# Cross-attention and FFN kernel: other PSUM banks for the last group's transposes, two softmax divisions on another engine

## The chip, the cores and the metric

The kernel runs on one core of a Trainium2 chip. The metric is the device time of one execution in microseconds (us); before the change its median over three executions was 541.05 us (540.98 to 541.4). A core has five engines that each work through a queue of their own in order: TensorE (PE in the profile; its weight loads are the row PEld), VectorE (DVE), ScalarE (ACT), GpSimd (POOL) and SyncE (SP, which here only issues transfers). They wait for each other by semaphores. TensorE writes its results to PSUM, here eight banks of 128 partitions x 512 float32; VectorE and ScalarE read them from there[...].

## The reference

Everything is float32. x is 2 x 2048 x 512, the context 2 x 128 x 512, with 16 heads of 32.

```python
h = layernorm(x)
q = h @ wq + bq; k = ctx @ wk + bk; v = ctx @ wv + bv      # 16 heads of 32
score = einsum('bhqd,bhkd->bhqk', q, k) / sqrt(32) * mask
score = where(score == 0, -1e9, score)
x = x + einsum('bhqk,bhkd->bqhd', softmax(score), v) @ wo + bo
y = real(ifft(fft(layernorm(x)) @ w_complex)) + bias
out = x + y
```

The kernel folds the two transforms and the complex matrix into one real 512 x 512 matrix m_ffn at its start.

## The kernel before

The 4096 rows of x are eight groups of four tiles of 128 rows. For each tile, TensorE computes the scores of all 16 heads against the 128 keys into two allocations of PSUM (two banks each), one for each half of the heads. The class Softmax handles one half (128 x 8 x 128): `masked` (VectorE, L334) multiplies scores by the mask into an SBUF tile w; `maxima` (VectorE, L341 to L344) replaces zeros and finds the row minima of the negated scores; `exponentials` (ScalarE, L350) makes eight activations with their sums; `divided` takes the reciprocal of the sums on VectorE (L362) and multiplies w by it on GpSimd (L363).

`transposed_weights` (L369) then turns the weights with TensorE, head group g by head group g (four transposes of 128 x 128 into one bank), and a copy moves each bank to pt in SBUF. Each g takes two heads from the first half and two from the second, in that order, so its third transpose is the first that needs the second half's division. `context` (L392) multiplies pt with v for a whole group of tiles, `Project` the result with wo; its `evict` adds to the residual x, to which `output_bias` (GpSimd, L418) has added bo. `ffn_statistics`, `ffn_norm` (L453; a norm on VectorE, L217, and the addition of bf on GpSimd, L458) and `ffn_transposes` (L461) prepare the second part, and `Ffn` multiplies by m_ffn, adds (VectorE, L503) and stores.

PSUM is divided into three pools: ps_sc with two allocations of two banks for scores, ps_tp with two of one bank for transposes, ps_mm with two of one bank for everything that accumulates. An allocation is handed out anew when its last reader is done.

The order of the work on each engine is the order in which the code issues it; no planner changes it. While a tile's softmax runs on VectorE, ScalarE and GpSimd, TensorE does the projections and FFN of earlier groups and the transposes of the tile before. In the helper `slot` (L720), `mid_a` is work issued behind the first matmul chain of a tile and ahead of the transposed weights of the tile before; at that place `masked` of the first half has been issued, and that of the second not. The last group (index 7) is written out by hand from L1092 on, without `slot`, except for its tile 0. There is no scores work to fill TensorE behind its tile 3, so the transposes of that tile's weights, the contexts, the projections and the FFN of the group follow each other alone:

```python
    w[1].exponentials()
    f_p[2].pe(between=[(ffn_transposes, p, 3, nc.vector)])
    f_p[2].evict()
    w[1].divided()
    output_bias(last)
    run(f_p[3])
```

For the last weights the kernel takes two allocations of ps_sc and uses each one's two banks for two head groups (L1158 to L1162); copies alternate between ScalarE (g = 0, 2) and VectorE (g = 1, 3).

Of the kernel before, what the change touches and what calls it, by code (L numbers as in the profile page):

```python
# [9 lines left out]
FP = mybir.dt.float32  # L10
# [4 lines left out]
P = 128  # L15
# [7 lines left out]
def kernel(  # L23
# [34 lines left out]
    nc = tc.nc  # L58
# [5 lines left out]
    NC = D // P  # L64
    NR = P // DH
# [10 lines left out]
    ps_sc = ctx.enter_context(  # L76
        tc.tile_pool(name="ps_sc", bufs=2, space=bass.MemoryType.PSUM)
    )
    ps_tp = ctx.enter_context(
        tc.tile_pool(name="ps_tp", bufs=2, space=bass.MemoryType.PSUM)  # L80
    )
    ps_mm = ctx.enter_context(
        tc.tile_pool(name="ps_mm", bufs=2, space=bass.MemoryType.PSUM)
    )
    HD = D // 2
    HC = NC // 2
# [91 lines left out]
    nc.sync.dma_start(bf, ffn_b.partition_broadcast(P))  # L178


    def transpose_rows(dst, src, name, eng, spare=False):

        pool, tag = (ps_mm, "mm") if spare else (ps_tp, "tp")
        ps = pool.tile([P, NC, P], FP, tag=tag, name=f"tp_{name}")
        for c in range(NC):
            nc.tensor.transpose(ps[:, c, :], src[:, c * P : (c + 1) * P], ident)  # L186
        if eng is nc.scalar:
            nc.scalar.copy(dst, ps)  # L188
        else:
            eng.tensor_copy(dst, ps)  # L190
# [77 lines left out]
    def query_transposes(i, t):  # L268
        if t == 0:
            xnTs[i] = big_tile("xnT", 1, f"xnT_{i}")  # L270
        transpose_rows(
            xnTs[i][:, :, t * P : (t + 1) * P], rels[i][t], f"a{i}_{t}", nc.scalar
        )
# [50 lines left out]
    class Softmax:  # L324
# [31 lines left out]
                    accum_out=self.den[:, h : h + 1],  # L356
                )

        def divided(self):
            w = self.w  # L360
            rden = small.tile([P, HH], FP, tag="rden", name=f"rden_{self.n}")
            nc.vector.reciprocal(rden, self.den)  # L362
            nc.gpsimd.tensor_tensor(  # L363
                w, w, rden.unsqueeze(2).to_broadcast([P, HH, K]), ALU.mult
            )

# [47 lines left out]
    def output_bias(i):  # L414

        xs = groups[i]
        for t in range(TG):
            nc.gpsimd.tensor_tensor(xs[:, t, :], xs[:, t, :], bo, ALU.add)  # L418
# [39 lines left out]
        nc.gpsimd.tensor_tensor(xt, xt, bf, ALU.add)  # L458
        norms[i, t] = n

    def ffn_transposes(i, t, eng=nc.scalar, spare=False):  # L461
        nTs[i, t] = work.tile([P, NC, P], FP, tag="nT", name=f"nT_{i}_{t}")
        transpose_rows(nTs[i, t], norms.pop((i, t)), f"f{i}_{t}", eng, spare)

# [250 lines left out]
    def begin(i, t):  # L715
        sc = scores(i, t)
        weights[i, t] = [Softmax(i, t, hf, sc[hf]) for hf in range(2)]
        return weights[i, t]
# [124 lines left out]
    w = begin(0, 0)  # L843
# [20 lines left out]
    w = begin(0, 1)  # L864
# [21 lines left out]
    w = begin(0, 2)  # L886
# [19 lines left out]
    w = begin(0, 3)  # L906
# [32 lines left out]
    w = begin(1, 0)  # L939
# [29 lines left out]
    for i in range(1, last - 1):  # L969
        p, pp, n, nn = i - 1, i - 2, i + 1, i + 2  # L970
# [12 lines left out]
        if i > 1:  # L983
            load_rows(nn)
            load_mask(n)
            load_residual(p)
            slot(
                i,
                0,
                [f_pp[1], f_pp[2], q[1]],  # L990
                turned=(p, TG - 1),
                early=[(ffn_transposes, pp, 2)],
                pool=[(relative, nn, t, nc.gpsimd) for t in range(TG)],
                on_b=[(ffn_norm, pp, 3), (query_statistics, nn, 0, 2)],
                on_c=[(query_statistics, nn, 2, TG)],
                end=[(context, p, 0, 2)],
            )
# [3 lines left out]
            second,  # L1001
            turned=(i, 0),
            early=[(context, p, 2, NC)] + if_pp((ffn_transposes, pp, 3)),
            pool=[(output_bias, p)],
            on_b=[(query_norm, nn, 0), (query_norm, nn, 1)],
# [8 lines left out]
            on_b=[(ffn_norm, p, 0), (query_norm, nn, 2), (query_norm, nn, 3)],  # L1014
            on_c=[(ffn_statistics, p, 1)],
            end=[(ffn_transposes, p, 0)],
        )
        slot(
# [14 lines left out]
    i, n, p, pp = last - 1, last, last - 2, last - 3  # L1033
# [4 lines left out]
    f = [Ffn(pp, t) for t in range(TG)]  # L1038
# [17 lines left out]
        pool=[(output_bias, p)],  # L1056
# [12 lines left out]
        [o[2], o[3], f_p[0]],  # L1069
        turned=(i, 2),  # L1070
        pool=[(ffn_norm, p, 0)],
        mid_a=[(ffn_transposes, p, 0)],
        on_a=[(ffn_statistics, p, 1)],
        on_b=[(ffn_norm, p, 1), (ffn_statistics, p, 2), (ffn_statistics, p, 3)],
        end=[(ffn_transposes, p, 1)],
# [1 line left out]
    i, p, pp = last, last - 1, last - 2  # L1077
    o = [Project(p, t) for t in range(TG)]
    f = f_p
# [5 lines left out]
        turned=(p, TG - 1),  # L1085
        late=True,
        pool=[(ffn_norm, pp, 2)],
        mid_a=[(ffn_transposes, pp, 2)],
        on_a=[(ffn_norm, pp, 3)],
        mid_c=[(ffn_transposes, pp, 3, nc.scalar, True)],  # L1090
    )
    w = begin(i, 1)  # L1092
    w[0].masked()
# [17 lines left out]
    old = w  # L1111
    w = begin(i, 2)
    w[0].masked()
    old[1].divided()
    o[1].pe()
    w[0].maxima()
    ffn_norm(p, 0)
# [17 lines left out]
    w = begin(i, 3)  # L1135
# [16 lines left out]
    w[1].exponentials()  # L1152
    f_p[2].pe(between=[(ffn_transposes, p, 3, nc.vector)])
    f_p[2].evict()
    w[1].divided()
    output_bias(last)
    run(f_p[3])
    free = [  # L1158
        ps_sc.tile([P, 2, NC, K], FP, tag="sc", name=f"tpw_last_{hf}")
        for hf in range(2)  # L1160
    ]
    banks = [free[g // 2][:, g % 2] for g in range(NC)]  # L1162
    for g in range(NC):
        transposed_weights(
            last, TG - 1, g, g + 1, nc.vector if g % 2 else None, banks
# [3 lines left out]
    f = [Ffn(last, t) for t in range(TG)]  # L1169
# [56 lines left out]
```

## Time and profile before

| | |
|---|---|
| median of three executions | 541.05 us |
| the profiled execution | 541.23 us |
| its span, first to last instruction | 539.0 us |
| TensorE clock granted | 1.00 |
| TensorE, VectorE, ScalarE, GpSimd busy | 98, 81, 64, 61% of the span |
| scores of group 7, tile 0 | from 439.90 us |
| first context matmul of group 7 | 502.51 us |

In rows of the timeline, the columns are the start in us from the span's start, the duration in us, engine, line, operation, the tile written and the tiles read with their shapes, and how many instructions were merged into the row; in brackets stands the idle time of the engine just before, and what ended it. A chain of waits is followed back from the last instruction: each step goes to what released it. Its rows have start, duration, engine and what.

By stages: from 441.0 to 452.5 VectorE is busy for 11.24 of 11.5 us; from 465 to 482 TensorE for 16.04 of 17.0; from 482 to 497 TensorE for 15.0 of 15.0 and VectorE for 13.34; from 497 to 502.5 TensorE for 3.86 of 5.5; from 502.5 to 539 TensorE for 33.15 of 36.5.

### The profile page before, as it was taken

The numbers are of one execution on the slowest core, as the hardware profiler recorded it, in microseconds if no ns is written. First come the engines' busy times: TensorE is split into PE (matmuls) and PEld (weight loads), VectorE is DVE, ScalarE is ACT, GpSimd is POOL, SyncE is SP. The second block draws the span as 40 slices with busy tenths as digits, with TensorE's granted clock in tenths as the row PEclk, the third lists the DMA queues.
The fourth block names the chain that finished last, engine by engine and source line by source line (L and its number), as shares of the span: only waits on it lengthen the run. The fifth ranks groups of instructions, "written<-read, shape, count | busy, mean of one in ns | idle before, by whom it ended". The sixth has DMA issues, their size and how long they took to land.

```text
span 539.0 us, 8776 instructions
## 1 busy us (share of the span) xinstructions
PE 526.0 (98%) x3005; PEld 293.4 (54%) x3005; DVE 437.2 (81%) x617; ACT 342.3 (64%) x1299; POOL 330.0 (61%) x268
## 2 busy tenths in 40 slices
PE   8979999999999999999999999999999999999897
PEld 7745567455545555455545555455545554455344
DVE  4698888799987998879887998879967898987251
ACT  3376786676677676666677676666676667666210
POOL 3246768935895459735895459735764466866450
PEclk9999999999999999999999999999999999999999
DMA  8960203000510015000610015000312001201002
GB/s 309 385 224 0 76 4 99 1 0 2 195 41 2 19 52 184 0 21 1 196 40 0 21 51 184 1 21 0 118 41 76 23 20 48 91 1 60 19 0 79
DMA packets 22992, 36.49 MB, mean 68 GB/s; under 512 B 2202, under 2 KB 6562, under 8 KB 22948
## 3 DMA queue, kind: packets, MB, share of 16 engines
q1 hardware_dynamic: 22260, 34.75, 18.7%
q10 hardware_dynamic: 688, 1.18, 0.6%
q8 instruction: 24, 0.39, 0.3%
q14 instruction: 20, 0.16, 0.1%
HBM read 27.53 MB, written 8.39 MB: 67 GB/s over the span
## 4 chain that ended last, share of the span: by engine, by line
PE 83%; DVE 10%; ACT 3%; POOL 2%; issue 1%; POOLq 0%; ACTq 0%; DVEq 0%
PE o L200 20%; PE q L200 16%; PE y L200 16%; PE tpw L380 9%; PE c L402 6%; PE sc L315 5%; PE tp_f L186 3%; PE tp_a L186 3%; ACT w L350 2%; DVE w L341 2%; DVE w L334 2%; DVE nmax L343 2%; POOL w L363 1%; PE k L547 1%; PE v L200 1%; DVE st_a L209 1%
## 5 line engine op out<-in xcount | busy, mean ns | idle before, releaser
L350 ACT ACTIVATE w<-w,nmax 128x128 f32<-128x128 f32 x512 | 198.3, 395 | 16.0 <-DVE nmax L344 15.0
L363 POOL TENSOR_TENSOR w<-w,rden 128x1024 f32<-128x1024 f32 x64 | 123.9, 1935 | 84.9 <-DVE rden L362 69.3
L200 PE MATMUL o<-wo,cT 128*128 128x512 f32 x256 | 115.3, 594 | 0.0
L200 PE MATMUL q<-xnT,wq 128*128 128x512 f32 (+1 forms) x256 | 112.0, 582 | 2.6 <-ACT qT L293 1.5
L200 PE MATMUL y<-m_ffn,nT 128*128 128x512 f32 x248 | 112.0, 594 | 0.2 <-DVE x L503 0.2
L387 ACT COPY pt<-tpw 128x512 f32<-128x512 f32 x120 | 64.3, 587 | 60.0 <-PE tpw L380 60.0
L350 ACT ACTIVATION_READ_ACCUMULATOR w<-w,nmax 128x1 f32 x512 | 99.2, 194 | 0.0
L341 DVE SCALAR_TENSOR_TENSOR w<-w 128x1024 f32<-128x1024 f32 x64 | 88.8, 1387 | 0.9
L334 DVE TENSOR_TENSOR w<-sc,mask 128x1024 f32<-128x1024 f32 x64 | 77.5, 1212 | 13.9 <-PE sc L315 13.6
L343 DVE TENSOR_REDUCE nmax<-w 128x8 f32<-128x1024 f32 x64 | 78.1, 1220 | 2.2
L380 PEld LDWEIGHTS tpw<-ident,w 128*128 128x128 f32 x496 | 57.7, 141 | 33.6 <-issue 29.3
L200 PEld LDWEIGHTS q<-xnT,wq 128*128 128x128 f32 x256 | 46.3, 190 | 48.6 <-issue 40.2
L200 PEld LDWEIGHTS o<-wo,cT 128*128 128x128 f32 x256 | 46.2, 190 | 47.5 <-issue 46.1
L200 PEld LDWEIGHTS y<-m_ffn,nT 128*128 128x128 f32 x248 | 44.6, 190 | 44.6 <-issue 43.8
L380 PE MATMUL tpw<-ident,w 128*128 128x128 f32 x496 | 65.2, 273 | 2.0 <-POOL w L363 1.0
L458 POOL TENSOR_TENSOR x<-x,bf 128x512 f32<-128x512 f32 x32 | 50.4, 1576 | 15.0 <-DVE norm_f L217 15.0
L213 POOL TENSOR_SCALAR rstd_f<-mv_f 128x1 f32<-128x1 f32 x32 | 18.1, 564 | 67.0 <-DVE mv_f L210 67.0
L418 POOL TENSOR_TENSOR x<-x,bo 128x512 f32<-128x512 f32 x32 | 46.9, 1494 | 0.0
L234 POOL TENSOR_SCALAR rel<-rows 128x512 f32<-128x512 f32 x26 | 42.2, 1638 | 1.4 <-PE tp_a L186 1.4
L315 PEld LDWEIGHTS sc<-kT,qT 32*128 32x128 f32 x1024 | 31.5, 186 | 15.1 <-issue 12.8
L188 ACT COPY nT<-tp_f 128x512 f32<-128x512 f32 x29 | 16.9, 583 | 34.3 <-PE tp_f L186 34.2
L362 DVE RECIPROCAL rden<-den 128x8 f32<-128x8 f32 x64 | 12.6, 197 | 31.9 <-ACT w L350 31.7
(99 smaller groups left out, 550.6 us busy)
## 6 DMA issues: line engine op xcount, KB each, us to landing
rows<-in_x_dram SPq DMA_DIRECT2D x32, 256.0 KB, 4.3
x<-in_x_dram SPq DMA_DIRECT2D x32, 256.0 KB, 5.1
out_dram<-x SPq DMA_DIRECT2D x31, 256.0 KB, 2.0
mask<-in_mask_Bx1xSxS_fk_dram SPq DMA_DIRECT2D x8, 256.0 KB, 5.8
wk<-in_L_xattn_wk_w_dram ACTq DMA_DIRECT2D x2, 512.0 KB, 6.3
wq<-in_L_xattn_wq_w_dram SPq DMA_DIRECT2D x1, 1024.0 KB, 7.8
wr<-n_L_ffn_w_freq_real_dram SPq DMA_DIRECT2D x2, 512.0 KB, 5.2
wi<-n_L_ffn_w_freq_imag_dram SPq DMA_DIRECT2D x2, 512.0 KB, 7.4
```

The costliest lines, as they stand in the source:

```text
L200: nc.tensor.matmul(ps, lhs(c), rhs(c), start=(c == 0), stop=(c == NC - 1))
L234: eng.tensor_scalar(d, xt, xt[:, 0:1], None, ALU.subtract)
L315: nc.tensor.matmul(sc[r // 2][:, r % 2, g, :], qTs[i][rows, g, t * P : (t + 1) * P], kT[rows, g, b * K : (b + 1) * K], start=True, stop=True,)
L334: nc.vector.tensor_tensor(self.w, self.sc.rearrange("p r g k -> p (r g) k"), self.mrow, ALU.mult)
L341: nc.vector.scalar_tensor_tensor(w, w, 0.0, w, ALU.is_equal, ALU.subtract)
L343: nc.vector.tensor_reduce(self.nmax, w, AX.X, ALU.min)
L350: nc.scalar.activation(w[:, h, :], w[:, h, :], AF.Exp, bias=self.nmax[:, h : h + 1], scale=-UNIT, accum_out=self.den[:, h : h + 1],)
L363: nc.gpsimd.tensor_tensor(w, w, rden.unsqueeze(2).to_broadcast([P, HH, K]), ALU.mult)
L380: nc.tensor.transpose(ps[:, r, :], ws[r // 2].w[:, (r % 2) * NC + g, :], ident)
L387: nc.scalar.copy(dst, ps)
L418: nc.gpsimd.tensor_tensor(xs[:, t, :], xs[:, t, :], bo, ALU.add)
L458: nc.gpsimd.tensor_tensor(xt, xt, bf, ALU.add)
```

## The change

Three things change.

- In the last group, `divided` of the second half of tile 1 (L1114) and of tile 3 (L1155) multiplies on VectorE instead of GpSimd. The reciprocal was on VectorE already.
- The last tile's weights are turned through four allocations: head groups 0 and 1 take the first bank of each of two score allocations, 2 and 3 an allocation of ps_tp each.
- Two of the norm transposes, in tile 3 of group 6 (L1072) and in tile 0 of group 7 (L1088), go through the first bank of a score allocation instead of one of ps_tp. Elsewhere `spare` means what it did: none is ps_tp, and for group 5's tile 3 (L1090) it is ps_mm, now given by name.

```diff
-    def transpose_rows(dst, src, name, eng, spare=False):
-        pool, tag = (ps_mm, "mm") if spare else (ps_tp, "tp")
-        ps = pool.tile([P, NC, P], FP, tag=tag, name=f"tp_{name}")
+    def transpose_rows(dst, src, name, eng, spare=None):
+        if spare is ps_sc:
+            ps = ps_sc.tile([P, 2, NC, P], FP, tag="sc", name=f"tp_{name}")[:, 0]
+        else:
+            pool, tag = (ps_mm, "mm") if spare else (ps_tp, "tp")
+            ps = pool.tile([P, NC, P], FP, tag=tag, name=f"tp_{name}")
...
-        def divided(self):
+        def divided(self, eng=nc.gpsimd):
             w = self.w
             rden = small.tile([P, HH], FP, tag="rden", name=f"rden_{self.n}")
             nc.vector.reciprocal(rden, self.den)
-            nc.gpsimd.tensor_tensor(
+            eng.tensor_tensor(
                 w, w, rden.unsqueeze(2).to_broadcast([P, HH, K]), ALU.mult
             )
...
-        mid_a=[(ffn_transposes, p, 0)],
+        mid_a=[(ffn_transposes, p, 0, nc.scalar, ps_sc)],
...
-        mid_a=[(ffn_transposes, pp, 2)],
+        mid_a=[(ffn_transposes, pp, 2, nc.scalar, ps_sc)],
         on_a=[(ffn_norm, pp, 3)],
-        mid_c=[(ffn_transposes, pp, 3, nc.scalar, True)],
+        mid_c=[(ffn_transposes, pp, 3, nc.scalar, ps_mm)],
...
     w[0].masked()
-    old[1].divided()
+    old[1].divided(nc.vector)
     o[1].pe()
     w[0].maxima()
...
     f_p[2].evict()
-    w[1].divided()
+    w[1].divided(nc.vector)
     output_bias(last)
     run(f_p[3])
     free = [
         ps_sc.tile([P, 2, NC, K], FP, tag="sc", name=f"tpw_last_{hf}")
         for hf in range(2)
     ]
-    banks = [free[g // 2][:, g % 2] for g in range(NC)]
+    banks = [bank[:, 0] for bank in free] + [
+        ps_tp.tile([P, NR, P], FP, tag="tp", name=f"tpw_last_{g}")
+        for g in range(HC, NC)
+    ]
```

More of the change, by code (lines that the diff above doesn't have):

```diff
@@ L459, in ffn_norm, with ffn_transposes @@
         norms[i, t] = n
-    def ffn_transposes(i, t, eng=nc.scalar, spare=False):
+    def ffn_transposes(i, t, eng=nc.scalar, spare=None):
         nTs[i, t] = work.tile([P, NC, P], FP, tag="nT", name=f"nT_{i}_{t}")
```

## The prediction

> **What bounds the kernel now.** I read the busy shares first, then the chain of work that ended last, then each engine's rows in order of time around the places that the diff touches.
>
> ```profile
> PE 526.0 (98%) x3005; PEld 293.4 (54%) x3005; DVE 437.2 (81%) x617; ACT 342.3 (64%) x1299; POOL 330.0 (61%) x268
> ```
>
> TensorE is busy almost throughout, so only the places where it stands still, or where the chain leaves it, can give time. The chain through the last group:
>
> ```profile
> 468.56 2.77 POOL w L363
> ...
> 471.38 0.87 PE tpw L380 x6
> ...
> 480.88 1.11 PE sc L315 x32
> 482.01 1.22 DVE w L334
> ...
> 493.52 3.20 ACT w L350 x16
> ...
> 497.12 1.87 POOL w L363
> ...
> 499.04 0.45 PE tpw_last L380 x2
> 499.52 0.59 ACT pt L387
> ...
> 502.58 3.62 PE c L402 x32
> ```
>
> Both divisions that the change moves stand on it (468.56 and 497.12), and so do the copies between the last transposes. From 482.01 to 493.4 the chain is VectorE's queue, row after row without a gap; from 502.58 to the end it is TensorE alone. The stalls themselves, in TensorE's and VectorE's rows:
>
> ```profile
> 471.38 0.87 PE L380 MATMUL tpw<-ident,w 128*128 128x128 f32 x6 [0.96 <-POOL w L363]
> 480.38 0.20 DVE L362 RECIPROCAL rden<-den 128x8 f32<-128x8 f32 x1 [0.70 <-ACT w L350]
> 482.01 1.22 DVE L334 TENSOR_TENSOR w<-sc,mask 128x1024 f32<-128x1024 f32 x1 [1.43 <-PE sc L315]
> 499.04 0.44 PE L380 MATMUL tpw_last<-ident,w 128*128 128x128 f32 x2 [0.28 <-POOL w L363]
> 500.15 1.09 PE L380 MATMUL tpw_last<-ident,w 128*128 128x128 f32 x8 [0.68 <-ACT pt L387]
> 501.93 0.66 PE L380 MATMUL tpw_last<-ident,w 128*128 128x128 f32 x4 [0.68 <-ACT pt L387]
> ```
>
> The two 0.68s fall before g=1 and g=3. Bank 1 is the second half of the allocation that bank 0 lies in, and waits for bank 0's copy although it is another bank; the same for 3 behind 2.
>
> **Part 1, the division of tile 1's second half on VectorE (L1114).** Nothing is added but the engine changes: one 128x1024 operation with two SBUF inputs leaves POOL (2.76 us here) and enters VectorE's queue before w[0].maxima. The trace has no such multiplication on VectorE; the nearest row is L341, the same size with its inputs in SBUF, 1.21 us when POOL is quiet. Its bounds are 1.19 (fastest L341) and 2.36 (slowest, behind POOL); I take 1.20, as POOL's rows are empty from 468.16 until the next norm. It runs 468.45 to 469.65. TensorE's third transpose goes at 470.26, right behind its second, instead of 471.38: 1.12 earlier, and so through o[2] and o[3] to tile 3's scores, which end at about 480.8 instead of 481.97.
>
> Behind the division on VectorE stand maxima, the norm, masked, an addition and the statistics, all 1.2 later. L344 gives 0.32 back: it took 0.49 at 470.86 against 0.17 elsewhere, because it waited for POOL's division, now gone. So the second half's maxima end 0.84 later (477.88). ScalarE's exponentials started at 477.16 and now start at 478.0, take their 3.18 and end at 481.18; the reciprocal follows, and masked of tile 3 goes at 481.33. Gain at that point: 482.01 - 481.33 = **0.68**, not 1.12; what ends last there is ScalarE, no longer the scores. Late next on POOL: a bias addition and tile 2's two divisions, by 0.84; the second then ends at 484.23, where TensorE comes to use it at 484.15 + 0.22, so it costs nothing as long as that 0.1 holds. Bounds of this part: 1.12 gained if ScalarE were not late, and 1.2 lost if the division simply lengthened VectorE's stretch.
>
> **Part 2, the division of tile 3's second half (L1155).** POOL needed 0.14 + 1.90 behind the reciprocal (ends 496.95 and 498.99). On VectorE it costs 1.2, but POOL is now not empty: the four additions of output_bias no longer queue behind this division, and start as soon as the first half's division ends. Such a case stands in the trace, VectorE's row and then POOL's:
>
> ```profile
> 280.84 2.07 DVE L341 SCALAR_TENSOR_TENSOR w<-w 128x1024 f32<-128x1024 f32 x1
> 280.54 5.95 POOL L418 TENSOR_TENSOR x<-x,bo 128x512 f32<-128x512 f32 x4
> ```
>
> The VectorE operation waits out the first addition (1.24, a quarter of the undisturbed 4.95 at 498.94: to 281.78), then runs 1.13 to 282.91, and POOL goes on after it (5.95 instead of 4.95). Here: the first half's division ends 2.05 behind its reciprocal's end (494.10), so at 496.15; the first addition at 497.39; VectorE's division is ready at 496.97, waits 0.42 and ends at 497.39 + 1.13 = 498.52, against 498.99. But TensorE itself reaches the third transpose no sooner than 498.38 + 0.22 = 498.60, so without part 1 the gain is 499.04 - 498.60 = 0.44; with everything ahead of it moved by 0.68, f_p[3] ends 0.9 sooner and it is the division that ends last, at 498.52 - 0.68 = 497.84; with the 0.05 that its release takes, the third transpose goes at 497.89, which is 499.04 - 0.68 - 0.47: **0.47**. Bounds: 0.9 if POOL happened to be between two additions, -0.7 if it waited for a whole second one. The output bias itself ends near 501.7; its reader is the addition at 509.93, so it stays covered by 5 us.
>
> [...] by the rows an uncontended VectorE operation is 1.20 against 1.90 to 2.76, and a contended one still ends 0.47 sooner than POOL's. I take the rows.
>
> **Part 3, four allocations for the last weights (L1158).** Same instructions, other banks: 0 and 1 become the first bank of each of two score allocations, 2 and 3 the two transpose banks, whose last readers (f_p[3]'s norm copy at 494.02 and a ScalarE copy near 492) are long done. The two waits before g=1 and g=3 go. Now 499.04 to 502.51, 3.47 us, lies between the third transpose and the first context matmul. After: 14 transposes at 0.109 (eight take 0.87 in the chain) = 1.53, and 0.14 for the hand-over that the rows show (502.37 to 502.51): 1.67. Gain **1.80**. The copies must keep up: with the third transpose at T, g=0 is complete at T+0.45 and copied by ScalarE at T+1.06, before the contexts' T+1.67; g=1's copy on VectorE follows f_p[3]'s addition and ends at T+1.62, needed at T+2.6; g=3's at T+2.45, needed at T+4.4. If the copies were not ready, the cover would be 0.6 us thin for g=0, nothing else.
>
> **Part 4, two norm transposes through a score allocation (L1072, L1088).** The next transposed weights get both transpose banks and lose a wait of 0.24 at 431.13 and of 0.29 at 445.87. The wait added is for masked of the first half, over at 427.8 and 442.3, when TensorE gets there at 429.85 and 444.54. After the first, scores land 0.15 sooner (the next norm, ending 439.18, holds the rest), VectorE had 0.22 to spare before masked, and then:
>
> ```profile
> 442.85 1.52 DVE L217 TENSOR_SCALAR norm_f<-x,mv_f,rstd_f 128x512 f32<-128x512 f32 x1
> ```
>
> A norm takes 0.54 undisturbed; this one waits for POOL's division (442.19 to 444.08), whose start doesn't depend on TensorE. So it ends at 444.37 whatever comes sooner. After the second, VectorE's queue runs full from 444.29 until f[3] waits for it at 452.4. I take **0**; bounds 0 and 0.5.
>
> **Sum.** 0.68 + 0.47 + 1.80 + 0 = 2.95 on the profiled span: 539.0 to 536.05. That execution took 541.23, 0.18 above the median of 541.05, and what lies around the span doesn't change: 541.05 - 2.95 = **538.1 us**.
>
> **Rivals.**
> - *Part 1 is swallowed* (18%): VectorE's stretch from 482 is the bound, and tile 2's late POOL work runs into it: a norm and a 0.1 us cover stand next to POOL's division at 484.2. For it: contended rows of 0.4 to 1.1 us on both engines there; against: the lateness found above. Without the 0.68 it is 538.8, and 539.3 if another 0.5 of such waits comes in.
> - [...] (6%): the last division waits for more than one bias addition. One more costs 1.24 (539.3), all four 3.7 (541.8). Against it: the row at 280.84, which got in after one.
> - *The banks don't part* (4%): the waits before g=1 and g=3 stay, by another dependency. 538.1 + 1.8 = 539.9. Against: g=2, in another allocation, followed g=1 without a wait.
> - *Part 4 gives more* (6%): the 0.5 of removed waits arrives; 537.6.
> - *Slower: the score allocation that part 4 takes is the second half's* (4%). The two norm transposes would wait for the second half's masked, over at 432.77 and 448.09: stalls of 2.92 and 3.55. The first passes wholly to VectorE, which then waits for the scores; of the second 1.8 is covered by f[2]'s addition at 451.75. 2.92 + 1.75 - 2.95 gives 542.8. It decides once the stalls that pass exceed 2.95 + 1.1. Against: with two allocations in turn, and an odd one between, the one that comes next each time is the half that was read first.
>
> **Chances and range.** The forecast has 62%, its own range 537.4 to 538.7. With the swallowed part 1 and the better part 4 it makes 86%; the range to hold 8 in 10 is 537.1 to 539.6. A run tells 0.2%, 1.1 us, from no change: faster is below 539.97. The forecast, the swallowed part 1, the better part 4, the banks (just)[...] make 0.89; [...] shares of unknowns make 0.06 for no change; the slower rival and some unknown 0.05.
>
> **What would show it.** Right: VectorE rows at L363 of about 1.2 (tile 1) and 1.5 (tile 3, wait included); no wait for POOL at tile 1's transposes; tile 3's masked released by ScalarE's exponentials, about 0.7 sooner; sixteen last transposes with at most one short wait after the second, contexts 1.67 after the third; an unchanged distance from contexts to the end. Wrong: a VectorE division above 2 us, a TensorE wait of 3 us at a norm transpose, masked of tile 3 at 482 or later, or last copies on which the contexts wait.

## The result and the profile after

The changed kernel takes 538.27 us (median of six executions, 538.15 to 538.36) against 541.3 us for the kernel before on the same chip: a ratio of 0.9944, 95% interval 0.9931 to 0.9956, or 3.0 us less. The forecast was 538.1. The profiled execution has a span of 536.1 us against 539.0. Line numbers are four higher after the change (L363 is L367, L334 is L338); in each version below they follow its own edit.

The chain through the last group, from tile 1's division to the first contexts:

```profile
468.40 1.23 DVE w L367
...
472.05 0.17 DVE nmax L348
...
477.74 0.18 DVE nmax L348
...
478.03 3.20 ACT w L354 x16
...
481.25 0.20 DVE rden L366
481.46 1.09 DVE w L338
...
497.77 1.90 PE tpw_last L384 x16
499.67 3.62 PE c L406 x32
```

GpSimd has left the chain. Between tile 1's division and tile 3 the chain is now VectorE and then ScalarE; TensorE's scores, which stood in front of tile 3's masked before (480.88, then 482.01), are no longer in it. The sixteen last transposes are one piece, where the chain had three with two copies between them. From the first context matmul to the end it is 36.5 us in both kernels (502.51 to 539.0, 499.60 to 536.1).

TensorE's rows at tile 1's transposes and at the end, then GpSimd's and VectorE's around the last division:

```profile
469.99 1.04 PE L384 MATMUL tpw<-ident,w 128*128 128x128 f32 x8
...
497.61 2.06 PE L384 MATMUL tpw_last<-ident,w 128*128 128x128 f32 x16
499.60 3.69 PE L406 MATMUL c<-pt,v 128*32 128x512 f32 x32
...
495.46 5.95 POOL L422 TENSOR_TENSOR x<-x,bo 128x512 f32<-128x512 f32 x4
...
496.33 1.47 DVE L367 TENSOR_TENSOR w<-w,rden 128x1024 f32<-128x1024 f32 x1
```

The 0.96 us wait at tile 1 is gone. VectorE's division takes 1.23 where GpSimd is idle and 1.47 where it adds the bias: it starts inside the first addition, as L341 did at 280.84, and GpSimd's four additions take 5.95 instead of 4.95.

Executions differ by up to 0.7 us in when they reach the last group, through what comes ahead of it, and a row's absolute time can't be compared across kernels to better than that. Below, times in the last group are therefore counted from one row: VectorE's addition for o[0], at 465.56 before and 465.51 after, just ahead of tile 2. Counted so, by each version's profiled execution:

| kernel | tile 3's masked | third of the last transposes | first context matmul |
|---|---|---|---|
| before | 16.45 | 33.48 | 36.95 |
| changed | 15.86 | one piece | 34.09 |
| banks alone | 16.44 | 33.48 | 35.16 |
| tile 1's division alone | 15.86 | 32.88 | 36.81 (granted clock 0.50 just before) |
| tile 3's division alone | 16.45 | 33.03 | 36.48 |
| norm transposes alone | 16.45 | 33.48 | 36.95 |

### The profile page after: what moved, and what is told of

It reads as the page before. It is cut to its first block, busy times and chain, and to the rows that moved or that the text cites. A ratio compares the mean times of both kernels' runs of the same rounds, so it can differ in the third digit from the quotient of the medians.

```text
span 536.1 us, 8773 instructions
## 1 busy us (share of the span) xinstructions
PE 525.3 (98%) x3005; PEld 293.2 (55%) x3005; DVE 439.4 (82%) x619; ACT 342.2 (64%) x1299; POOL 326.5 (61%) x266
## 4 chain that ended last, share of the span: by engine, by line
PE 76%; DVE 17%; ACT 5%; POOL 1%; issue 1%; ACTq 0%; POOLq 0%; DVEq 0%
PE y L204 16%; PE o L204 16%; PE q L204 15%; PE tpw L384 8%; PE c L406 5%; PE sc L319 5%; ACT w L354 4%; DVE w L345 4%; DVE nmax L347 3%; DVE w L338 3%; PE tp_a L190 3%; PE tp_f L190 2%; PE k L551 1%; PE v L204 1%; DVE norm_f L221 1%
## 5 line engine op out<-in xcount | busy, mean ns | idle before, releaser
L367 POOL TENSOR_TENSOR w<-w,rden 128x1024 f32<-128x1024 f32 x62 | 119.3, 1924 | 83.4 <-DVE rden L366 67.2
L345 DVE SCALAR_TENSOR_TENSOR w<-w 128x1024 f32<-128x1024 f32 x64 | 88.7, 1386 | 0.9
L338 DVE TENSOR_TENSOR w<-sc,mask 128x1024 f32<-128x1024 f32 x64 | 77.4, 1211 | 12.4 <-PE sc L319 11.8
```

Of the source, the lines that this page charges most:

```text
L338: nc.vector.tensor_tensor(self.w, self.sc.rearrange("p r g k -> p (r g) k"), self.mrow, ALU.mult)
L345: nc.vector.scalar_tensor_tensor(w, w, 0.0, w, ALU.is_equal, ALU.subtract)
L367: eng.tensor_tensor(w, w, rden.unsqueeze(2).to_broadcast([P, HH, K]), ALU.mult)
```

## The experiments

The theory: the parts add up along one chain, each by what it takes from the wait that ends last. The main rival: moving work between GpSimd and VectorE brings nothing, and all of the gain is the banks.

**Each part alone.** The first is the new `banks` list and nothing else:

```diff
-    banks = [free[g // 2][:, g % 2] for g in range(NC)]
+    banks = [bank[:, 0] for bank in free] + [
+        ps_tp.tile([P, NR, P], FP, tag="tp", name=f"tpw_last_{g}")
+        for g in range(HC, NC)
+    ]
```

> The kernel before with only the last weights' four allocations changed. Own theory (the parts add up along one chain): 1.8 us faster than before; the third last transpose still waits for GpSimd's division at 499.0, the other thirteen follow without a wait, and the first context matmul starts 1.67 behind the third transpose instead of 3.47. Rival (moving the divisions brought nothing, all of the 3 us is here): 2.9 us faster. Rival (the waits come from elsewhere and stay): 0.

Measured 539.13 us against 541.23, ratio 0.9959 (0.9947 to 0.9971). TensorE's rows:

```profile
498.88 1.75 PE L380 MATMUL tpw_last<-ident,w 128*128 128x128 f32 x14 [0.29 <-POOL w L363]
500.56 0.64 PE L402 MATMUL c<-pt,v 128*32 128x512 f32 x4
```

One wait for GpSimd, and then fourteen without another; the contexts follow 1.68 behind the third transpose, 1.79 sooner than before. The medians differ by 2.1; the interval of the ratio is 1.6 to 2.9 us, and 1.79 lies in it. The 3 us are not all here.

The next two give `divided` its argument, as in the change, and use it in one place each:

```diff
-    old[1].divided()
+    old[1].divided(nc.vector)
```

> The kernel before with only tile 1's second-half division on VectorE. Own theory: 0.68 us faster; TensorE loses its 0.96 wait at 471, but tile 3's masked is then released by ScalarE's exponentials and starts at 481.35 instead of 482.01. Rival ([...]): 0, or up to 0.5 slower. Rival (TensorE's wait is what counts): 1.1 faster.

Measured 540.82 us, ratio 0.9997 (0.9986 to 1.0008). The median stands between two kinds of execution: eight of the fourteen took 540.2 to 540.85, six took 542.09 to 542.42 with a lower granted TensorE clock; the last section returns to them. The eight have a median of 540.46, 0.74 less than the 541.2 of the forty executions of the kernel before, on the same chip, whose clock did not fall. The profile is of the second kind, but up to 501.6 its rows are undisturbed. VectorE's, and then TensorE's:

```profile
481.65 0.20 DVE L362 RECIPROCAL rden<-den 128x8 f32<-128x8 f32 x1 [0.70 <-ACT w L350]
481.77 1.17 DVE L334 TENSOR_TENSOR w<-sc,mask 128x1024 f32<-128x1024 f32 x1
...
498.79 0.44 PE L380 MATMUL tpw_last<-ident,w 128*128 128x128 f32 x2 [0.41 <-POOL w L363]
```

Masked of tile 3 starts 0.59 sooner and the third transpose 0.60 sooner (table). Neither 0 nor 1.1: the wait for ScalarE's exponentials stands right ahead of masked, as expected.

```diff
-    w[1].divided()
+    w[1].divided(nc.vector)
     output_bias(last)
```

> The kernel before with only tile 3's second-half division on VectorE. Own theory: 0.44 us faster; the division waits for a bias addition on GpSimd and lasts 1.4 to 1.6, but TensorE, not the division, then sets the third last transpose, at 498.60. Rival ([...]): 0. Rival (it gets in at once, and TensorE is no limit): 0.8 faster.

Measured 540.6 us, ratio 0.9987 (0.998 to 0.9993). VectorE's row and then TensorE's:

```profile
497.16 1.47 DVE L363 TENSOR_TENSOR w<-w,rden 128x1024 f32<-128x1024 f32 x1
...
498.55 0.64 PE L380 MATMUL tpw_last<-ident,w 128*128 128x128 f32 x4
```

The contexts start 0.47 sooner. The first four of the last transposes are one piece, and the division has ended (498.63) when the third is due (498.77), so TensorE and not the division sets them.

The norm transposes, with the new `transpose_rows`:

```diff
-        mid_a=[(ffn_transposes, p, 0)],
+        mid_a=[(ffn_transposes, p, 0, nc.scalar, ps_sc)],
...
-        mid_a=[(ffn_transposes, pp, 2)],
+        mid_a=[(ffn_transposes, pp, 2, nc.scalar, ps_sc)],
```

> The kernel before with only the two norm transposes through a score allocation. Own theory: 0 (within 0.2 us); TensorE loses its waits of 0.24 and 0.29 and waits longer for VectorE at 452.5 instead, by the 0.4 that it gained. Rival (the removed waits arrive): 0.4 to 0.5 faster.

Measured 541.1 us, ratio 0.9995 (0.9987 to 1.0003): nothing that can be told from 0. In the last group: 0.59 + 0.47 + 1.79 + 0 = 2.85, and the changed kernel has 36.95 - 34.09 = 2.86. The parts add up; the medians' 3.0 is 0.14 more, less than executions of one kernel differ.

**Bank or allocation.** The two allocations of the kernel before, with neighbours in different ones:

```diff
-    banks = [free[g // 2][:, g % 2] for g in range(NC)]
+    banks = [free[g % 2][:, g // 2] for g in range(NC)]
```

> The kernel before, with the same two score allocations for the last weights in another order: head groups 0 and 2 in the first, 1 and 3 in the second. Theory (a transpose waits for the copy of the allocation, not of its bank, so neighbours must not share one): 1.2 us faster than before; no wait ahead of g=1, about 0.45 ahead of g=2 and 0.1 ahead of g=3. Rival (only fresh banks or the transposes' own pool help): 0. Rival (the order is all, and the copies are always in time): 1.8.

Measured 540.25 us against 541.63, ratio 0.9975 (0.9964 to 0.9986). TensorE's rows:

```profile
499.31 0.87 PE L380 MATMUL tpw_last<-ident,w 128*128 128x128 f32 x6 [0.29 <-POOL w L363]
500.42 1.20 PE L380 MATMUL tpw_last<-ident,w 128*128 128x128 f32 x8 [0.24 <-ACT pt L387]
501.55 0.64 PE L402 MATMUL c<-pt,v 128*32 128x512 f32 x4
```

The wait before g=1 is gone; one is left before g=2, for the copy of g=0 in the same allocation. The same four banks in another order give 1.22 of the 1.79 (35.73 in the table's count). So a transpose does wait for the reader of its allocation, though that reads another bank. These waits are the program's own, by semaphore; whether the chip would need them, no run here shows.

**Where the norm transposes' gain stays.** TensorE's row at the chain for f[3], in the kernel before and in the changed one:

```profile
452.54 0.67 PE L200 MATMUL y<-m_ffn,nT 128*128 128x512 f32 x1 [0.16 <-DVE x L503]
```

```profile
452.49 1.10 PE L204 MATMUL y<-m_ffn,nT 128*128 128x512 f32 x2 [0.56 <-DVE x L507]
```

The 0.40 that TensorE gained it waits for VectorE here. Two runs take 1.0 us of waiting out of VectorE's queue ahead of this place (the norm at 442.85 takes 1.52 beside GpSimd's division of 442.19 to 444.08, against 0.54 at 471.26), without and with the new norm transposes. They move the second half's `masked` ahead of that norm:

```diff
         while carried:
             carried.pop(0)()
+        if both:
+            halves[1].masked()
         call(pool)
...
             halves[0].exponentials()
-            halves[1].masked()
+            if not both:
+                halves[1].masked()
             finish(first)
```

with `both=True` in the last group's tile 0.

> The kernel before; in tile 0 of the last group VectorE does the second half's masked before the norm[...]. Theory (VectorE's queue sets tile 0, and TensorE has only 0.16 of waiting there without the change's norm transposes): 0.15 us faster, VectorE reaching its addition for f[2] about 1 us sooner. Rival (VectorE's wait passes on in full): 1.0 faster. Rival (another row takes the wait): 0.

Measured 541.7 us against 541.63, ratio 1.0 (0.9991 to 1.0008); from the norm that VectorE does in group 6's tile 3 (437.33 before) to the addition for o[0] it is 28.18 instead of 28.23. VectorE does reach its addition for f[2] 1.0 us sooner (counted from the same norm), but TensorE had only the 0.16 to gain. Of the expected 0.15 the rows show 0.05, too little for the times to tell.

> The changed kernel with the same reordering of VectorE in tile 0. Theory: what the two norm transposes saved on TensorE stands as a wait of 0.56 at 452.5 and now comes free: 0.5 us faster than the changed kernel, so 3.5 faster than before. Rival (the norm transposes save nothing that can be used): as without them, 0.15, so 3.1 faster than before.

Measured 538.56 us, ratio 0.9941 (0.9929 to 0.9954), 3.07 us faster than before and hardly faster than the changed kernel's 3.0: a miss. The same stretch is 27.78 instead of 28.23: TensorE's 0.45 does come free and reaches o[0]. Then it is lost again. VectorE's rows in tile 1 and at its second division:

```profile
456.62 1.78 DVE L345 SCALAR_TENSOR_TENSOR w<-w 128x1024 f32<-128x1024 f32 x1
...
459.70 1.11 DVE L348 TENSOR_SCALAR nmax<-nmax 128x8 f32<-128x8 f32 x1
...
465.26 0.69 DVE L443 TENSOR_TENSOR x<-o,x 128x512 f32<-128x512 f32 x1 [0.57 <-PE o L204]
...
468.16 0.20 DVE L366 RECIPROCAL rden<-den 128x8 f32<-128x8 f32 x1 [0.16 <-ACT w L354]
468.40 1.23 DVE L367 TENSOR_TENSOR w<-w,rden 128x1024 f32<-128x1024 f32 x1
```

The reciprocal waits 0.16 for ScalarE's exponentials, which could start only behind the small operation at 459.70. It takes 1.11 while GpSimd adds the bias, as in the changed kernel (1.12, against 0.17 at 464.42, where GpSimd is idle), and counted from the norm it starts only 0.12 sooner than there: L345 ahead of it, beside GpSimd's division, takes 1.78 instead of 1.45. Of 0.45 there is 0.19 left at the contexts. In the changed kernel the two chains all but tie at that reciprocal, which its own rows hardly show: ScalarE's exponentials end at 468.06, the reciprocal starts at 468.17, and no wait stands there.

**What VectorE's time in tile 2 is worth.** In the changed kernel tile 1's second half is divided by two engines:

```diff
-    old[1].divided(nc.vector)
+    old[1].divided_apart()
...
+        def divided_apart(self):
+            w = self.w
+            rden = small.tile([P, HH], FP, tag="rden", name=f"rden_{self.n}")
+            nc.vector.reciprocal(rden, self.den)
+            lead = w.rearrange("p (r g) k -> p r g k", g=NC)[:, :, :HC, :]
+            by = rden.rearrange("p (r g) -> p r g", g=NC)[:, :, :HC]
+            nc.vector.tensor_tensor(
+                lead, lead, by.unsqueeze(3).to_broadcast([P, 2, HC, K]), ALU.mult
+            )
+            for h in (2, 3, 6, 7):
+                nc.scalar.activation(
+                    w[:, h, :], w[:, h, :], AF.Identity, scale=rden[:, h : h + 1]
+                )
```

> The changed kernel, with tile 1's second-half division shared: VectorE divides the four heads of head groups 0 and 1, which TensorE needs first, and ScalarE, idle there for 2 us, the other four. Theory (VectorE's queue and ScalarE's exponentials behind it set tile 3's start, one for one): VectorE's part is 0.67 instead of 1.23, tile 3's masked starts at 480.8 instead of 481.37, and the kernel is 0.45 us faster than the changed one, 3.4 faster than before. Rival (the scores set tile 3's start, VectorE's time there is covered): 0 against the changed kernel, 2.95 faster than before.

Measured 538.22 us against 541.63, ratio 0.9937 (0.9924 to 0.9949), 3.41 faster. VectorE's and ScalarE's rows:

```profile
469.02 0.69 DVE L377 TENSOR_TENSOR w<-w,rden 128x512 f32<-128x512 f32 x1
...
481.44 1.19 DVE L338 TENSOR_TENSOR w<-sc,mask 128x1024 f32<-128x1024 f32 x1
...
469.02 1.28 ACT L381 ACTIVATE w<-w,rden 128x128 f32<-128x128 f32 x4 [0.35 <-DVE rden L374]
```

VectorE's part is 0.54 shorter (1.23 to 0.69), masked of tile 3 starts 0.55 sooner (15.31) and the contexts 0.53 sooner (33.56): one for one.

**Both, and a third step.** First the changed kernel itself, beside them:

> The changed kernel once more, as the measure for the two versions run with it. All theories: 3.0 us faster than before.

Measured 538.32 us against 541.14, ratio 0.9941 (0.9927 to 0.9955).

> The changed kernel with both further edits: VectorE's second masked of tile 0 ahead of the norm, and tile 1's division shared with ScalarE. Theory (tile 0's 0.45 is taken back in tile 1 by ScalarE's exponentials[...]; only 0.2 is left; the shared division gives its 0.5): 0.7 us faster than the changed kernel, 3.7 faster than before. Rival (the exponentials of tile 1 now set everything, so the 0.2 goes too): 3.5. Rival (the two add in full): 4.0.

Measured 537.74 us, ratio 0.993 (0.9914 to 0.9946): 3.4 us faster than before and 0.58 faster than the changed kernel beside it. From the norm in group 6's tile 3 to the contexts it takes 61.59 against 62.32, the expected 0.7. Its median is the lowest of all runs here; measured against the kernel before beside it, the shared division alone gained as much (3.41), and only the rows put this version 0.20 ahead of that one (61.59 against 61.79). For the third step ScalarE takes over a small operation of `maxima`, since its exponentials keep their 0.39 us each beside GpSimd's work (in the changed kernel 0.39 at 462.00, beside the bias additions, and at 474.27, where GpSimd is idle):

```diff
-    w[0].maxima()
+    w[0].maxima(nc.scalar)
...
+            if eng is nc.scalar:
+                nc.scalar.mul(self.nmax, self.nmax, UNIT)
...
```

> The same, and the last step of tile 1's first maxima (128x8, times a constant) on ScalarE[...]. Theory: tile 1's exponentials start about 0.9 sooner and the whole 0.45 of tile 0 comes through: 1.0 faster than the changed kernel, 4.0 faster than before. Rival (something else than that wait holds the exponentials): as without it, 0.7 and 3.7.

Measured 539.1 us, ratio 0.9954 (0.9939 to 0.9968): 1.4 us worse than without it, outside both expectations. ScalarE's row, and then TensorE's:

```profile
459.36 0.21 ACT L349 ACTIVATE nmax<-nmax 128x8 f32<-128x8 f32 x1 [4.64 <-DVE nmax L347]
...
460.10 1.49 PE L423 MATMUL c<-pt,v 128*32 128x512 f32 x11 [1.57 <-ACT cT L431]
```

The step itself takes 0.21 beside GpSimd's additions. But it stands in ScalarE's queue ahead of the copies of two contexts. It waits there for VectorE's minima until 459.36, the copies behind it are late, and TensorE's next contexts wait 1.57 for the PSUM banks that they hold. The edit should have been issued behind those copies; that was not tried, so whether the whole 0.45 of tile 0 can be had is open.

**The bias addition beside the last division.** The changed kernel, leaving out the output bias of the last group:

```diff
-    output_bias(last)
```

> The changed kernel without the four additions of the output bias to the last group (its last four tiles lack that bias). Theory (the last division waits for one addition, but TensorE comes only just before it ends): the division lasts 1.2 instead of 1.47, and the last transposes go without a wait, so that the contexts start 0.1 to 0.2 us sooner behind the reciprocal. Rival ([...]): the contexts start 0.27 or more sooner. Rival (the 0.27 has another cause): the division still lasts 1.47.

One execution, 538.24 us, read for its rows: the division takes 1.22 instead of 1.47, and from the last reciprocal to the contexts it takes 499.72 - 496.37 = 3.35 instead of 3.50.

```profile
496.60 1.22 DVE L367 TENSOR_TENSOR w<-w,rden 128x1024 f32<-128x1024 f32 x1
...
497.88 1.91 PE L384 MATMUL tpw_last<-ident,w 128*128 128x128 f32 x16
```

The wait is for GpSimd's addition, and it costs 0.15 of its 0.25, because TensorE comes only a little before the division ends.

## Why the prediction was right

It gave 2.95 us; the rows of the last group have 2.86, the spans 2.9 and the medians 3.0. By its steps:

- **Part 1**, 0.68 forecast, 0.59 measured. The mechanism held in each link: the division at 468.40 took 1.23 (1.20 forecast), L344's 0.49 went back to 0.17, the exponentials started at 478.03 (478.0) and released masked. The size was off by 0.09, and the term is how late the exponentials start: 0.92 by the rows (12.52 behind o[0]'s addition instead of 11.60), not 0.84. Half of that is a slip in the sum, for 1.20 less 0.32 is 0.88; the rest is that the division held up the next operation by 1.25 and not 1.20. The POOL work of tile 2 that I feared came as worked out: its second division ended at 484.28, and TensorE's transposes, whose third needs it, ran from 484.22 in one piece (GpSimd's row, then TensorE's):

```profile
482.38 1.90 POOL L367 TENSOR_TENSOR w<-w,rden 128x1024 f32<-128x1024 f32 x1
...
484.22 1.04 PE L384 MATMUL tpw<-ident,w 128*128 128x128 f32 x8
```

- **Part 2**, 0.47 forecast (0.44 alone), 0.47 measured alone; beside the other parts it is 0.48, what they leave of the 2.86. The row at 280.84 gave the contended price: 1.55 forecast with its wait, 1.47 measured.
- **Part 3**, 1.80 forecast, 1.79 measured.
- **Part 4**, 0 forecast, 0 measured, and the 0.40 stands in TensorE's wait at 452.5.

Of the rivals, the slower one didn't come. TensorE's two norm transposes in the score allocation start without a wait:

```profile
429.80 0.60 PE L190 MATMUL tp_f<-ident,norm_f 128*128 128x128 f32 x4
...
444.48 0.61 PE L190 MATMUL tp_f<-ident,norm_f 128*128 128x128 f32 x4
```

The chances that the prediction lists for a faster kernel add up to 0.93, not to its 0.89. Beside GpSimd's addition the last division lost 0.25 (1.47 against 1.22), but both moved divisions were worth about half a microsecond, because the operation itself is a third shorter (1.23 against 1.90) and left the chain sooner.

## What to carry to other kernels

Cost each edit on the wait that ends last at its place, and follow the second chain too: tile 1's division freed 1.12 us on TensorE and gave 0.59, since the work queued behind it on the new engine came late by 0.92. Where two transposes in a row shared an allocation here, the second waited 0.68 us for the first one's copy though the banks differed; spread neighbours over allocations. The chain that tied with the critical one (exponentials to 468.06, reciprocal from 468.17) showed no wait in the profile, and took back what the next edit gained (0.45 to 0.19 here).

## What the runs showed of the hardware

I had not expected TensorE's clock to fall inside the last group. In six of fourteen executions with tile 1's division alone, in one of thirteen with the second half's masked ahead of the norm, and in seven of 79 of the kernel before, the time was 1.4 to 2.0 us above the median of the others and the mean granted clock 0.996. The profiled executions of the first two are such. In the first, by stretches of 2 us, a row gives busy times and, in the third column from the end, the granted clock:

```profile
498.00:500.00 2.00, 0.92 (x6) 0.44 (x5) 0.69 (x1) 0.58 (x1) 2.00 (x3) 1.00 0.09 34
500.00:502.00 2.00, 1.32 (x10) 1.09 (x11) 0.69 (x1) 0.58 (x1) 2.00 (x2) 0.91 0.26 97
502.00:504.00 2.00, 2.00 (x12) 0.78 (x14) 0.69 (x1) 0.00 (x0) 1.64 (x2) 0.50 0.00 0
504.00:506.00 2.00, 2.00 (x16) 0.44 (x12) 0.00 (x0) 0.73 (x2) 0.00 (x0) 0.73 0.00 0
```

From 502 to 504 the granted clock is 0.50; by the 0.91 and 0.73 of the rows beside it, it stands so, as an estimate, from 501.6 to 505.05, 3.4 us, and the contexts take 4.84 instead of 3.69. From 498 to 502 TensorE was busy for only 2.24 of 4.0 us, with the waits for GpSimd and for the copies between; its longest single wait was 0.68. In the 3.4 us just ahead of the fall it was busy for 1.7, and in the second trace for 1.8 of the 3.4 us ahead of 502.5, from where the clock stands at 0.50 until 505.9 (estimated from the 0.63 and 0.52 granted in the stretches from 502 and from 504). In the 47 executions of kernels whose banks spread these transposes (all with the changed `banks`, and the interleaved one) it didn't happen. What sets the fall off, and why only some executions have it, no run here shows. That the removed stalls are what prevents the fall is the author's estimate from the counts, and not tested by itself. The counts alone don't decide it: the norm transposes alone (13 executions) and 20 of the 21 of tile 3's division alone keep both waits of 0.68 and kept the clock as well.

The twenty-first, of tile 3's division alone, took 557.6 us with a mean clock of 0.949; it has no trace, and its cause is open.
